# One semaphore per k-and-v buffer for the gathers of a graph attention kernel, in place of eight shared in turn

## The chip, the core and the metric

The kernel runs on one core of one Trainium2 chip. The metric is the device time of one execution in microseconds (us); lower is better. The engines of the core are named as in the profile: PE is the matrix engine's matmul side and PEld its weight loads, DVE is VectorE, ACT is ScalarE, POOL is GpSimd and SP is SyncE. Each engine runs its own instructions in order. Engines and transfers (DMAs) tell each other of finished work through semaphores: a counter that a finished instruction or transfer raises, and that another instruction waits for. A transfer raises its semaphore by 16 in all when it has landed.

## What is computed

A graph with 6250 nodes of 128 features and 206250 edges, sorted by receiver. For each edge, a weight vector comes out of two small networks on its 32 + 32 features; the query of its receiver, that weight and the key of its sender make one attention number for each of 8 heads; this scales the sender's value; the scaled values are summed by receiver, added to the node features and normalized.

```python
w_ij = jax.nn.silu(edge_feats @ rad_W1 + rad_b1) @ rad_W2 + rad_b2
w_ij = w_ij + (jax.nn.silu(chi_scalar @ sph_W1 + sph_b1) @ sph_W2 + sph_b2)
q_i = (node_feats @ Wq).reshape(-1, NUM_HEADS, HEAD_DIM)[receivers]
k_j = (node_feats @ Wk).reshape(-1, NUM_HEADS, HEAD_DIM)[senders]
alpha = (q_i * w_ij * k_j).sum(axis=-1) / jnp.sqrt(jnp.float32(HEAD_DIM))
alpha = alpha * cutoffs[:, None]
v_j = (node_feats @ Wv)[senders].reshape(-1, NUM_HEADS, HEAD_DIM)
out = jax.ops.segment_sum(alpha[..., None] * v_j, receivers, num_segments=n_nodes) / 16.0
x = _layernorm(x + out.reshape(-1, 128), axis=-1)
```

## The kernel before

**Work units.** 128 edges are a tile, four tiles are a quad (512 edges), four quads are a group. There are 403 quads. One execution first computes k and v of all nodes on PE and stores them as a table in memory (`kv_tab`, one row of 1 KB for each node), then runs one loop over the groups with four slots each, one quad a slot, written out by hand: what an engine does stands in its queue in the order of the program text.

**Gathers.** For each tile of a quad, POOL issues one indirect transfer that fetches 128 rows of `kv_tab` by the senders' indices (`gather`, L136). The rows of a quad go into one of `RING` = 16 buffers named `kv`. The function `gathers` issues a quad's four, 14 quads ahead in the program text (`AHEAD` = `RING` - 2). Each is also made to wait for a matmul of the quad that is then current ("no gather ahead of TensorE"), which is 14 quads earlier than the quad that it fetches, and a quad's first gather waits until VectorE has read the buffer's earlier content, which is that of 16 quads earlier. The first eight quads do not gather from `kv_tab`: for them 32 gathers fetch rows of x (tile `msg`), and k and v are computed on the spot.

**Row quads.** For 56 quads, spread between the quads 20 and 392 of the order, POOL gathers only three tiles. The 128 rows of the fourth are fetched by 128 transfers of one row each, 64 issued by SP and 64 by ACT (`load_rows`, tile `wide`). These signal one of eight semaphores of their own, `rows_0` to `rows_7`, and VectorE waits once for a quad's full count (L580), with `declare_fence` telling the layer that records the program that this wait stands for all of them.

**Semaphores of the gathers.** The recording layer gives all other transfers that POOL issues one of eight semaphores in turn, called lanes here. Two transfers of a lane are kept from being in flight together: a gather waits until the gather of eight before, on its lane, has landed. In the program before, the fast path has 1510 separate wait instructions on POOL in front of its 1556 gathers; each names a lane, and 389 of them also name a semaphore of VectorE (the buffer's earlier reader) besides. Where VectorE first reads a quad's rows (L583), it waits for the lanes of its four tiles, two to a wait instruction.

**Behind the gathers.** For each quad VectorE multiplies query and key (`multiply`, L583, tile `kq`), multiplies with the weight (L591), sums over each head (L593), scales (L597) and multiplies into the value (`messages`, L610). PE computes the first layers (L524), the query at the edges (L533, tile `pq`), the weight (L566 and L571, tile `pw`) and the sum by receiver (L622). ACT applies the activation (L554). In a slot, PE and ACT work on later quads than VectorE does.

The lines that the change touches, before:

Of the kernel before, what the change touches and what calls it, by code (L numbers as in the profile page):

```python
# [48 lines left out]
RING = 16  # L49
# [20 lines left out]
def gnn_kernel(ctx, tc, x, src, dst, weight, edges, rad_W1, rad_b1, rad_W2, rad_b2,  # L70
# [14 lines left out]
    nc = tc.nc  # L85
# [46 lines left out]
    def quad_of(name, bufs, width=D):  # L132
        return ep.tile([P, QT, width], F32, name=name, bufs=bufs)

    def gather(o, table, index):
        return nc.gpsimd.indirect_dma_start(  # L136
            out=o, out_offset=None, in_=table,
            in_offset=bass.IndirectOffsetOnAxis(ap=index, axis=0))
# [7 lines left out]
    row_done = {}  # L146
    rows_left = {SP: [], ACT: []}
    owed = {SP: 0, ACT: 0}
    row_sems = [tc.alloc_semaphore(f"rows_{n}") for n in range(ROW_SEMS)]
    row_count = [0] * ROW_SEMS  # L150

    def next_rows(engine, n):

        left = rows_left[engine]
        for _ in range(min(n, owed[engine])):
            row = next(left[0], None)
            while row is None:
                left.pop(0)
                row = next(left[0], None)
            row()  # L160
            owed[engine] -= 1
# [5 lines left out]
    def gathers(q, marks=()):  # L167

        kv = quad_of("kv", RING, 2 * D)
        for t in range(QT - 1 if q in row_quads else QT):  # L170
            o = gather(kv[:, t, :], kv_tab, src_i[:, q * QT + t:q * QT + t + 1])
            if marks:
                tc.add_manual_dep(o.ins, marks[t].ins.name, WAIT, reason="no gather ahead of TensorE")
        kv_of[q] = kv

    def load_rows(i):

# [37 lines left out]
    def kv_parts(q, t):  # L215

        if q not in row_quads:
            return [(t, kv_of[q][:, t, :])]
        return [(slice(0, QT - 1), kv_of[q][:, :QT - 1, :]), (slice(QT - 1, QT), row_of[q])]
# [90 lines left out]
    with tc.tile_pool(name="nodes", bufs=1) as nodes, \  # L310
# [154 lines left out]
        n = len(chunks)  # L465
# [45 lines left out]
        for q in order[XQ:AHEAD]:  # L511
            gathers(q)
# [5 lines left out]
    with tc.tile_pool(name="ps", bufs=1, space=PSUM) as pp, tc.tile_pool(name="loop", bufs=1) as lp:  # L518
# [19 lines left out]
        def after(o, mark, reason="one signal of TensorE a quad"):  # L538
            tc.add_manual_dep(o.ins, mark.ins.name, WAIT, reason=reason)
# [36 lines left out]
        def multiply(q, mark=None, t=slice(0, QT)):  # L576
            if t.start == 0:
                kq_of[q] = quad_of("kq", 3)
            if t.start == 0 and q in row_done:
                o = nc.vector.wait_ge(*row_done[q])  # L580
                tc.declare_fence(o.ins, group=f"rows_{q}")
            for u, kv in kv_parts(q, t):
                o = nc.vector.tensor_tensor(kq_of[q][:, u, :], pq_of[q][:, u, :], kv[:, :, :D],  # L583
                                            op=OP.mult)
                if mark is not None:
                    after(o, mark)
# [182 lines left out]
        q_at_edges(order[0])  # L769
        silus(order[1], first_layers(order[1]))  # L770
        multiply(order[0])
        marks = weigh(order[0])
        mark = marks[-1]
        seen = [mark] * 3
        for g in range(NG - 1):
            for slot, j in enumerate((0, 2, 1, 3)):
                q = g * NQ + j
# [29 lines left out]
                if i + AHEAD < len(order):  # L807
                    gathers(order[i + AHEAD], old[-QT:])
                multiply(order[i + 1], mark)
                messages(q, scores(q, marks=marks), marks=marks)  # L810
                if slot == 0:
# [24 lines left out]
                if g == NG - 2 and slot == 0:  # L836
                    wide_one_hots(order[-1])
                    n = nc.values_load(general, min_val=0, max_val=1)
# [20 lines left out]
        part_sums(g - 1)  # L859
        messages(a, scores(a, weighted=False))  # L860
        multiply(b, mark)
        normalize(g - 3, g - 2, sd)
        write_rows(len(written))
# [191 lines left out]
```

## Time and profile before

| | |
|---|---|
| median of three runs | 1994.42 us (1992.89 to 1995.7) |
| the profiled execution's own time | 1990.48 us |
| its span, first to last instruction | 1988.4 us |
| mean granted TensorE clock | 0.933 of full speed |
| busy PE / PEld / DVE / ACT / POOL | 1788.7 / 1494.6 / 1521.5 / 647.0 / 1474.3 us |
| gathers from `kv_tab` / of x | 1524 / 32, 946 / 957 ns of POOL each |

A busy PE is not PE at its peak, since the ends of matmuls are modelled. The grouped lines give, for a kind of instruction, its count, its total busy time, the mean of one in ns, and the time that the engine sat idle just before them, with what most often ended that idle time. Such a releaser is inferred: of the semaphores that an instruction waits for, it is the one that moved last by the profile, and an instruction whose waits were long met can still carry the name of one that happens to move often. In a timeline a row gives start, duration, engine, line, operation and tiles, and in brackets the idle time before it. In a table of windows "(x128)" is the number of instructions in a stretch of time.

### The profile page before, as it was taken

Reading aid. Unit: us, or ns where it says so; the run is one execution under the profiler, and the core shown is the slowest. Engines: PE = TensorE matmul, PEld = TensorE weight load, DVE = VectorE, ACT = ScalarE, POOL = GpSimd, SP = SyncE. Lnnn points to the kernel's source line nnn. Section 1 sums busy time; section 2 is a strip of 40 time slices with the busy share of each in tenths; the row PEclk is TensorE's granted clock in tenths of the full one; section 3 lists DMA queues with packets and bytes.
Section 4 is the critical chain, followed back from the end, with each engine's and each line's share of the span. In section 5 each row is a group of like instructions: output and inputs, shape, how many; then the busy total and the mean of one; then the engine's idle time right before and its main releaser. Section 6 shows DMA issues by size and latency. Waiting matters only on the chain. (4 is left out here: it accounts for less than half of the span.)

```text
span 1988.4 us, 58734 instructions
## 1 busy us (share of the span) xinstructions
PE 1788.7 (90%) x15990; PEld 1494.6 (75%) x15990; DVE 1521.5 (77%) x3411; ACT 647.0 (33%) x1360; POOL 1474.3 (74%) x1566
## 2 busy tenths in 40 slices
PE   9899989889987988989889889989989888988997
PEld 7787877777876777777777777767778777777776
DVE  6788888677877777777777777777777778777787
ACT  3233333332332332332333323323323333333343
POOL 7777766777777777777777777777777777777775
PEclk9899999988999999898999889999889999998998
DMA  9555545555554555555555555555555555555543
GB/s 342 154 151 155 146 146 147 144 150 152 148 155 144 156 157 147 154 151 151 152 147 153 144 155 146 156 145 156 155 145 155 144 154 151 150 154 145 156 142 91
DMA packets 153261, 305.51 MB, mean 154 GB/s; under 512 B 40300, under 2 KB 87260, under 8 KB 152924
## 3 DMA queue, kind: packets, MB, share of 16 engines
q0 software_dynamic: 74176, 201.95, 35.7%
q1 hardware_dynamic: 70080, 95.67, 15.0%
q10 hardware_dynamic: 8668, 4.08, 1.0%
q8 instruction: 127, 2.08, 0.4%
q14 instruction: 210, 1.72, 0.3%
HBM read 288.10 MB, written 13.46 MB: 152 GB/s over the span
## 5 line engine op out<-in xcount | busy, mean ns | idle before, releaser
L136 POOL DMA_INDIRECT kv<-kv_tab,src_i x1524 | 1441.8, 946 | 489.2 <-PE pw L571 185.0
L554 ACT ACTIVATE act<-ph,b 128x512 f32<-128x512 f32 x806 | 553.3, 687 | 1284.4 <-PE pq L533 677.9
L571 PE MATMUL pw<-w,act 128*128 128x128 f32 x6448 | 889.4, 295 | 0.0
L571 PEld LDWEIGHTS pw<-w,act 128*128 128x128 f32 x6448 | 810.4, 204 | 97.1 <-issue 81.7
L524 PE MATMUL ph<-feats,w 32*128 32x512 f32 x1612 | 544.0, 680 | 47.5 <-ACT act L554 46.1
L533 PE MATMUL pq<-q,hotT 32*128 32x128 f32 x3224 | 495.1, 295 | 8.7 <-DVE kq L583 8.6
L583 DVE TENSOR_TENSOR kq<-pq,kv 128x512 f32<-128x512 f32 (+1 forms) x403 | 270.5, 671 | 294.5 <-DMA kv<-kv_tab,src_i 147.6
L533 PEld LDWEIGHTS pq<-q,hotT 32*128 32x128 f32 x3224 | 414.9, 197 | 29.5 <-DVE kq L583 28.1
L593 DVE TENSOR_REDUCE side<-kq 128x32 f32<-128x512 f32 x403 | 280.1, 695 | 42.2 <-PE pw L571 0.5
L610 DVE TENSOR_TENSOR msg<-kv,side 128x512 f32<-128x512 f32 (+1 forms) x404 | 269.9, 668 | 43.2 <-DVE side L597 0.9
L591 DVE TENSOR_TENSOR kq<-pw,kq 128x512 f32<-128x512 f32 x403 | 274.6, 681 | 0.1
L524 PEld LDWEIGHTS ph<-feats,w 32*128 32x128 f32 x1612 | 150.5, 192 | 161.5 <-ACT act L554 94.9
L566 PE MATMUL pw<-brow,onesb 3*128 3x512 bf16 x403 | 160.7, 399 | 0.6 <-DVE kq L591 0.6
L622 PE MATMUL po<-msg,hot 128*32 128x128 f32 x3200 | 158.3, 296 | 0.0
L663 PE MATMUL pq<-part,to 128*128 128x128 f32 x200 | 49.1, 331 | 107.4 <-DVE kq L583 106.9
L663 PEld LDWEIGHTS pq<-part,to 128*128 128x128 f32 x200 | 33.1, 208 | 118.4 <-DVE kq L583 104.0
L597 DVE TENSOR_TENSOR side<-side,scale 128x32 f32<-128x32 f32 x400 | 80.0, 200 | 43.7 <-DVE side L593 1.4
L622 PEld LDWEIGHTS po<-msg,hot 128*32 128x32 f32 x3200 | 73.4, 113 | 38.9 <-issue 5.5
L263 DVE TENSOR_TENSOR hotT<-relb,side 128x512 f32<-128x512 bf16 x101 | 68.8, 681 | 0.0
L268 DVE TENSOR_TENSOR hot<-rel,side 128x512 f32<-128x512 f32 x100 | 68.1, 681 | 0.0
L257 PE MATMUL pq<-wq,xT 128*128 128x128 f32 x200 | 43.0, 299 | 18.9 <-DVE kq L583 18.6
L257 PEld LDWEIGHTS pq<-wq,xT 128*128 128x128 f32 x200 | 32.7, 205 | 23.0 <-DVE kq L583 22.9
(121 smaller groups left out, 823.9 us busy)
## 6 DMA issues: line engine op xcount, KB each, us to landing
wide<-kv_tab SPq DMA_DIRECT2D x3584, 1.0 KB
wide<-kv_tab ACTq DMA_DIRECT2D x3584, 1.0 KB
feats<-in_edges SPq DMA_DIRECT2D x101, 512.0 KB
kv<-kv_tab,src_i POOLq DMA_INDIRECT x1524
relb<-rel_lin SPq DMA_DIRECT2D x101, 128.0 KB
x<-in_x SPq DMA_DIRECT2D x101, 64.0 KB
out<-y SPq DMA_DIRECT2D x101, 64.0 KB
kv_tab<-kv SPq DMA_DIRECT2D x12, 512.0 KB
```

Of the source, the lines that this page charges most:

```text
L136: return nc.gpsimd.indirect_dma_start(out=o, out_offset=None, in_=table, in_offset=bass.IndirectOffsetOnAxis(ap=index, axis=0))
L524: return nc.tensor.matmul(act_of[q, i], w1[r0:r0 + R, :], feats_of[g][r0:r0 + R, c0:c0 + EQ], start=True, stop=True)
L533: o = nc.tensor.matmul(pq_of[q][:, t, :], hotT_of[g][b, t * P:(t + 1) * P], q_of[g][b, :], start=True, stop=True)
L554: o = nc.scalar.activation(act, act_of[q, i], AF.Silu, bias=b1[:, i:i + 1])
L566: nc.tensor.matmul(pw, onesb, brow.rearrange("p t d -> p (t d)"), start=True, stop=False)
L571: o = nc.tensor.matmul(pw[:, t, :], act_of[q, i][:, t * P:(t + 1) * P], w2[:, i, :], start=False, stop=(t == QT - 1 and i == 1))
L583: o = nc.vector.tensor_tensor(kq_of[q][:, u, :], pq_of[q][:, u, :], kv[:, :, :D], op=OP.mult)
L591: nc.vector.tensor_tensor(m, pw_of[q][:, t, :], m, op=OP.mult)
L593: o = nc.vector.tensor_reduce(alpha, m.rearrange("p t (h e) -> p t h e", e=HD), AX.X, OP.add)
L610: o = nc.vector.tensor_tensor(msg_of[q][:, u, :].rearrange("p t (h e) -> p t h e", e=HD), kv[:, :, D:].rearrange("p t (h e) -> p t h e", e ...
L622: o = nc.tensor.matmul(po_of[g][j * W:(j + 1) * W, :], hot_of[g][:, j * QT + t, :], msg_of[g * NQ + j][:, t, :], start=(t == 0), stop=(t = ...
L663: nc.tensor.matmul(ph[:, :D], to[:n, 0, :], part[:n, :], start=True, stop=(g == 0))
```

## The change

Each of the 16 `kv` buffers gets a semaphore of its own, `kv_0` to `kv_15`. All gathers of a quad raise its buffer's semaphore by 16 each, and they take no lane: the recording layer neither gives them one of its eight semaphores nor follows what depends on their landing. In their place VectorE waits once, ahead of a quad's first multiplication, until the buffer's semaphore has reached the count of the quad's last gather, as it does for the row transfers.

```diff
+    kv_sems = [tc.alloc_semaphore(f"kv_{n}") for n in range(RING)]
+    kv_count = [0] * RING
+    kv_done = {}
...
     def gathers(q, marks=()):
 
         kv = quad_of("kv", RING, 2 * D)
+        n = len(kv_done) % RING
         for t in range(QT - 1 if q in row_quads else QT):
             o = gather(kv[:, t, :], kv_tab, src_i[:, q * QT + t:q * QT + t + 1])
+            tc.no_tile_sem_insts.add(o.ins.name)
+            tc.add_to_no_dep_group(f"kv_{q}", o.ins)
+            o.then_inc(kv_sems[n], 16)
+            kv_count[n] += 16
             if marks:
                 tc.add_manual_dep(o.ins, marks[t].ins.name, WAIT, reason="no gather ahead of TensorE")
         kv_of[q] = kv
+        kv_done[q] = kv_sems[n], kv_count[n]
...
         def multiply(q, mark=None, t=slice(0, QT)):
             if t.start == 0:
                 kq_of[q] = quad_of("kq", 3)
-            if t.start == 0 and q in row_done:
-                o = nc.vector.wait_ge(*row_done[q])
-                tc.declare_fence(o.ins, group=f"rows_{q}")
+            for name, done in (("rows", row_done), ("kv", kv_done)):
+                if t.start == 0 and q in done:
+                    o = nc.vector.wait_ge(*done[q])
+                    tc.declare_fence(o.ins, group=f"{name}_{q}")
```

In the program as built, the order of the working instructions and of the transfers is the same on every engine; only waits differ. On POOL's fast path the separate wait instructions go from 1510 to 393. 379 of those that are left stand ahead of a quad's first gather and name two semaphores of VectorE: that of its engine, as before, and that of its queue, raised when the new wait of 16 quads earlier has passed. No gather from `kv_tab` waits for another gather any more. On VectorE, the lane waits ahead of L583 (734 that name two lanes and 56 that name one) give way to 395 waits for a `kv` semaphore, each of which raises the queue's own semaphore when met, and 395 waits for that one.

## The prediction, as put on record before the changed kernel was run

> **What bounds the kernel now.** I read the page first, then POOL's gathers stretch by stretch and one by one, then VectorE's waits.
>
> ```profile
> span 1988.4 us, 58734 instructions
> PE 1788.7 (90%) x15990; PEld 1494.6 (75%) x15990; DVE 1521.5 (77%) x3411; ACT 647.0 (33%) x1360; POOL 1474.3 (74%) x1566
> L136 POOL DMA_INDIRECT kv<-kv_tab,src_i x1524 | 1441.8, 946 | 489.2 <-PE pw L571 185.0
> L583 DVE TENSOR_TENSOR kq<-pq,kv 128x512 f32<-128x512 f32 (+1 forms) x403 | 270.5, 671 | 294.5 <-DMA kv<-kv_tab,src_i 147.6
> ```
>
> By the first line of busy times PE looks like the bound. But POOL's 74% hides something: 946 ns busy and 489.2 us / 1524 = 321 ns idle make 1.27 us for each gather, and 1556 of these (with the 32 of x) fill the whole span. The next rows are single gathers of POOL's timeline: the first three of all, then the first and the last of the final 20.
>
> ```profile
> 2.88 1.10 POOL L136 DMA_INDIRECT msg<-in_x,src_x  x1 [1.27 <-DMA src_x<-in_src]
> 4.28 0.94 POOL L136 DMA_INDIRECT msg<-in_x,src_x  x1 [0.30 <-issue]
> 5.53 0.95 POOL L136 DMA_INDIRECT msg<-in_x,src_x  x1 [0.30 <-issue]
> ...
> 1949.24 0.94 POOL L136 DMA_INDIRECT kv<-kv_tab,src_i  x1 [0.30 <-issue]
> ...
> 1973.00 0.94 POOL L136 DMA_INDIRECT kv<-kv_tab,src_i  x1 [0.30 <-issue]
> ```
>
> From 1949.24 to 1973.00 there are 19 steps: 1.2505 us each. The first gathers go at the same 1.25, so 0.95 of work and 0.30 of pause belong to a gather itself. 1555 steps of 1.2505 are 1944.5 us; from 2.88 to 1973.00 they took 1970.1. So POOL runs at its own pace from start to end, and lost only 25.6 us on the way. Is it what the others wait for? The first table counts gathers, the second L591, one for each quad.
>
> ```profile
> core 0: us, POOL busy (x), PEclk, DMA share, GB/s
> 70.00:230.00 160.00, 121.10 (x128) 0.99 0.52 154
> 230.00:455.00 225.00, 158.38 (x168) 0.93 0.51 147
> 455.00:900.00 445.00, 335.36 (x356) 0.94 0.52 151
> 900.00:1400.00 500.00, 375.17 (x397) 0.93 0.52 150
> ```
>
> ```profile
> 100.00:230.00 130.00, 21.11 (x31) 0.99 0.52 153
> 900.00:1400.00 500.00, 70.05 (x103) 0.93 0.52 150
> ```
>
> Early, while gathers are far ahead, a quad takes 130 / 31 = 4.19 us. Later it takes 500 / 103 = 4.85, and POOL's 1524 / 395 = 3.86 gathers a quad take 3.86 x 1.2505 = 4.82. VectorE then waits for rows (147.6 us at L583, above). So POOL sets the end; the 14.5 us from the last gather's end (1973.94) to 1988.4 are the last quads' work.
>
> **Where POOL's 25.6 us went.** In 70 to 230 nothing is lost (160 / 1.2505 = 128). In 230 to 455 there is room for 179.9 gathers and there are 168: 11.9 x 1.25 = 14.9 us. Two kinds of gap show. The first:
>
> ```profile
> 316.40 0.95 POOL L136 DMA_INDIRECT kv<-kv_tab,src_i  x1 [0.31 <-issue]
> ...
> 328.16 0.94 POOL L136 DMA_INDIRECT kv<-kv_tab,src_i  x1 [1.53 <-DMA kv<-kv_tab,src_i]
> ```
>
> These two are eight gathers apart, so of one lane, and the later one waited for a landing: the gather that POOL had finished issuing at 317.35 (316.40 + 0.95) had landed only shortly before 328.16. Eight gathers at 1.25 are 10.0 us, and a landing that takes longer stops POOL. The second kind:
>
> ```profile
> 282.71 0.95 POOL L136 DMA_INDIRECT kv<-kv_tab,src_i  x1 [3.28 <-DVE to L653]
> 424.50 0.95 POOL L136 DMA_INDIRECT kv<-kv_tab,src_i  x1 [1.00 <-PE pw L571]
> 958.87 0.94 POOL L136 DMA_INDIRECT kv<-kv_tab,src_i  x1 [1.71 <-DVE side L593]
> 1092.94 0.94 POOL L136 DMA_INDIRECT kv<-kv_tab,src_i  x1 [1.77 <-PE pw L571]
> 1226.52 0.94 POOL L136 DMA_INDIRECT kv<-kv_tab,src_i  x1 [1.16 <-DVE msg L610]
> 1492.69 0.94 POOL L136 DMA_INDIRECT kv<-kv_tab,src_i  x1 [1.17 <-DVE kq L583]
> 1626.52 0.94 POOL L136 DMA_INDIRECT kv<-kv_tab,src_i  x1 [1.53 <-issue]
> 1760.37 1.02 POOL L136 DMA_INDIRECT kv<-kv_tab,src_i  x1 [1.37 <-PE pw L571]
> ```
>
> From 958.87 on these stand 133.6 to 134.1 us apart, or twice that: every 106 gathers, which are 212 instructions of POOL with the wait in front of each. They follow the instruction count, so I read them as POOL's queue fetching its next block. Their pauses sum to 13.0 us, 10.6 beyond 8 x 0.30. The same step seen back from 282.71 falls at 149, in the stretch that lost nothing: with early landings POOL's queue has instructions prepared ahead and a fetch passes unseen. It hurts where the lane wait holds the queue back until just before the gather. That is an inference; the regular step is not.
>
> The rest, 25.6 - 10.6 = 15.0, is longer gathers and lane waits. The first gather alone is 0.15 over 0.95; I leave 1.0 for such and count 14.0 as lane waits.
>
> **The change, part by part.** The wait instructions on POOL (1510 to 393):
>
> ```profile
> L136 POOL DMA_INDIRECT kv<-kv_tab,src_i x1524: 940/946/1468, 43.3 to 1973.0; - x191
> L136 POOLq EVENT_SEMAPHORE  x1510: 17/17/43, 37.9 to 1966.1; - x189
> ```
>
> (ns: least, median, most.) At 17 ns beside a gather that runs they cost nothing, and the pause of 0.30 doesn't come from them: the first one stands at 37.9, while gathers from 4.28 on already go at 1.25. So the steady pace stays; I take 0 for it.
>
> Lane waits go: gain 14.0 us; at least the 14.9 of the early stretch less its two block fetches (3.28 + 1.00 - 0.60 = 3.7), so 11.2; at most 15.0.
>
> Block fetches: POOL's instructions a gather fall from 2 to about 1.25, so if each still cost what it does, 10.6 x 0.375 = 4.0 is gained; if the queue is far enough ahead, as before 230, all 10.6. I take 10.6, since nothing is left that holds the queue: the buffer's earlier reader is 16 quads back and the matmul 14.
>
> [...]
>
> VectorE: the waits at L583 remain two, but the second now waits for the first.
>
> ```profile
> L593 DVE TENSOR_REDUCE side<-kq 128x32 f32<-128x512 f32 x403 | 280.1, 695 | 42.2 <-PE pw L571 0.5
> L580 DVEq EVENT_SEMAPHORE  x56: 21/21/21, 170.6 to 1925.8; - x56
> ```
>
> L593 waits for VectorE's own L591, idle 42.2 / 403 = 0.105 us each: the bound above for one such turn, 395 x 0.105 = 41 us in all. Below it is nothing, since a wait met early passes beside running work, 21 ns as at L580. I take 0.1, but it lies in a quad's slack of 4.82 - 4.19 = 0.63 us, and PE, ACT and POOL don't wait for VectorE to issue gathers. On the path are only the last three quads: 0.3 us. If VectorE set the pace, the cost would be the 41.
>
> Sum: 14.0 + 10.6 - 0.3 = 24.3, from the profiled execution's own 1990.5 to 1966.2. That execution lies 3.9 under the median of 1994.4; carried over, **1970**.
>
> What is late next: quads must then go at 3.86 x 1.2505 = 4.82 without pauses, against 4.19 when fed, so POOL's own 0.95 + 0.30 remains the bound.
>
> **The rivals.**
>
> *Landing is a bound of its own.* The lanes hold POOL only where landings are late; without them more gathers may merely be under way, and VectorE waits at L583 instead. For it: the 10 us landing above, with the 16 transfer engines busy only 0.51 of the time on average.
>
> ```profile
> wide<-kv_tab SPq DMA_DIRECT2D x3584, 1.0 KB
> wide<-kv_tab ACTq DMA_DIRECT2D x3584, 1.0 KB
> ```
>
> A landing so late at half load means that some part of a gather queues behind other traffic, and these 7168 one-row transfers are the candidate. Against it: from 455 on, 1.25 to 1.26 us a gather was landed for over 1400 us. If the early stretch gains nothing, what stays is 14.0 - 11.2 = 2.8, and the six later fetches, 8.7 - 1.8 = 6.9: 9.7 us, so 1985.
>
> [...]
>
> [...]
>
> *Nothing changes.* The waits on POOL show 43 ns at most; were the gaps not the lanes', everything stays: 1994. Against it stands the row at 328.16, with a landing named as releaser and eight rows between.
>
> **How the numbers follow.** Forecast 0.62 (its own range 1965 to 1980, with the fetches' 4.0 to 10.6 and 1.5 of scatter as in the runs shown), landing-bound 0.19, crowding 0.11, nothing 0.08. All told the range is 1963 to 1991: it holds the forecast and nearly all of the landing-bound case, and leaves out crowding and nothing. Faster by over 0.2% (about what a measurement of this kernel tells from no change) 0.81, within it 0.08, slower 0.11.
>
> **What would show it.** In the profile after: POOL's last gather starts near 1949 (not 1973); 230 to 455 holds about 180 gathers; the gaps at every block of instructions are gone or under 0.5 us; the pause stays 0.30. The wait at L583 for landings is no more than now. I am wrong on the cause if POOL finishes early but the end doesn't move, which is the landing bound, or if gaps over 0.30 remain as many as they are, and wrong on VectorE's wait if quads take over 4.85 us while gathers have long landed.

## The result, and the profile after

The changed kernel takes 1966.8 us (median of four runs, 1966.19 to 1967.4) against 1993.89 us before (four runs, 1992.89 to 1995.7): a ratio of 0.9863, 95% interval 0.9846 to 0.988. The forecast was 1970, its own range 1965 to 1980, the whole range 1963 to 1991. The profiled execution took 1966.43 us; the sum of the prediction for it was 1966.2.

From the page of the changed kernel, the span, the busy times and two of the costliest groups (lines below L136 have moved down: the first multiplication is now L593, the second L601, the sum over heads L603):

```profile
span 1964.3 us, 57621 instructions
PE 1770.4 (90%) x15990; PEld 1480.0 (75%) x15990; DVE 1516.8 (77%) x3411; ACT 648.3 (33%) x1360; POOL 1476.0 (75%) x1566
L136 POOL DMA_INDIRECT kv<-kv_tab,src_i x1524 | 1442.6, 947 | 465.0 <-issue 198.8
L593 DVE TENSOR_TENSOR kq<-pq,kv 128x512 f32<-128x512 f32 (+1 forms) x403 | 269.8, 669 | 249.1 <-DVEq L590 110.0
```

The third line is where the time came from: POOL's idle time in front of its gathers fell from 489.2 to 465.0 us, which is 24.2, while a gather kept its length (946 to 947 ns). The last line is where it could have gone and did not: VectorE's wait for gathered rows, which was 147.6 us with the landing named as releaser, is 110.0 with the queue's own semaphore named (the turn behind the new wait at L590); all the idle time ahead of the first multiplication fell from 294.5 to 249.1.

POOL's gathers in the same stretches as before, and VectorE's second multiplication (one for each quad) in two of them:

```profile
core 0: us, POOL busy (x), PEclk, DMA share, GB/s
70.00:230.00 160.00, 121.13 (x128) 0.98 0.53 153
230.00:455.00 225.00, 170.16 (x180) 0.95 0.54 153
455.00:900.00 445.00, 336.34 (x357) 0.93 0.54 153
900.00:1400.00 500.00, 378.08 (x400) 0.93 0.54 152
```

```profile
230.00:455.00 225.00, 33.34 (x49) 0.95 0.54 153
900.00:1400.00 500.00, 70.73 (x104) 0.93 0.54 152
```

In 230 to 455 there are 180 gathers in place of 168, and 225 / 180 = 1.250 us is POOL's own pace. Every stretch now runs at it: 500 / 400 = 1.25. A quad takes 500 / 104 = 4.81 us late in the run, which is POOL's 3.86 x 1.2505 = 4.82 again.

The instructions of L136 (ns: least, median, most; then first and last start), POOL's timeline around the place where before had its longest pause, and the last gather:

```profile
L136 POOL DMA_INDIRECT kv<-kv_tab,src_i x1524: 942/946/1648, 44.2 to 1950.6; - x191
L136 POOLq EVENT_SEMAPHORE  x393: 17/43/43, 39.4 to 1931.5; - x197
```

```profile
281.48 0.95 POOL L136 DMA_INDIRECT kv<-kv_tab,src_i  x1 [0.30 <-PE pw L580]
282.73 0.94 POOL L136 DMA_INDIRECT kv<-kv_tab,src_i  x1 [0.30 <-DVEq L590]
...
1950.56 0.95 POOL L136 DMA_INDIRECT kv<-kv_tab,src_i  x1 [0.30 <-issue]
```

Of the 38 pauses over 0.34 us that POOL had before (24.3 us beyond the 0.30 of each, added up along its timeline) none is left after the first gather. The bracket names change from gather to gather while the number stays 0.30: this is the case in which a releaser is only the semaphore that moved last, and the number says that nothing was waited for.

What the 38 pauses were can be read from the trace of the kernel before, by matching each gather with the increments of its lane's semaphore (a trace lacks some increments; the last one recorded is taken as the landing). No gather there starts less than 0.76 us after the landing of the gather eight before. In 28 of the 38 pauses it starts 0.76 to 0.79 us after it: these are the lane waits, 13.4 us beyond the 0.30 of each. The eight pauses that the prediction lists at every 106th gather start 3.34 to 3.40 us after that landing: 10.6 us. At four further steps of 106 gathers the landing had come early enough for that, at most 5.7 us after the issue, and nothing is lost. Two pauses, 0.3 us together, fit neither (one of them stands at a step of 106). In the changed kernel landings are no earlier: from 455 us on, a quad has landed 6.5 to 7.3 us (medians of three stretches) after POOL's part in its last gather ended, and at most 10.5, where the kernel before has medians of 5.7 to 6.4. POOL no longer waits for them.

### The profile page after: what moved, and what is told of

Its sections match the earlier page's. It is cut to its first block, busy times and chain, and to the rows that moved or that the text cites. A ratio compares the mean times of both kernels' runs of the same rounds, so it can differ in the third digit from the quotient of the medians.

```text
span 1964.3 us, 57621 instructions
## 1 busy us (share of the span) xinstructions
PE 1770.4 (90%) x15990; PEld 1480.0 (75%) x15990; DVE 1516.8 (77%) x3411; ACT 648.3 (33%) x1360; POOL 1476.0 (75%) x1566
## 3 DMA queue, kind: packets, MB, share of 16 engines
q8 instruction: 127, 2.08, 0.5%
## 5 line engine op out<-in xcount | busy, mean ns | idle before, releaser
L136 POOL DMA_INDIRECT kv<-kv_tab,src_i x1524 | 1442.6, 947 | 465.0 <-issue 198.8
L580 PEld LDWEIGHTS pw<-w,act 128*128 128x128 f32 x6448 | 802.0, 203 | 96.3 <-issue 79.0
L542 PE MATMUL pq<-q,hotT 32*128 32x128 f32 x3224 | 487.6, 292 | 5.9 <-DVE kq L593 5.8
L593 DVE TENSOR_TENSOR kq<-pq,kv 128x512 f32<-128x512 f32 (+1 forms) x403 | 269.8, 669 | 249.1 <-DVEq L590 110.0
L542 PEld LDWEIGHTS pq<-q,hotT 32*128 32x128 f32 x3224 | 408.8, 195 | 19.7 <-DVE kq L593 15.5
L603 DVE TENSOR_REDUCE side<-kq 128x32 f32<-128x512 f32 x403 | 279.9, 695 | 43.6 <-DVE kq L601 1.4
L601 DVE TENSOR_TENSOR kq<-pw,kq 128x512 f32<-128x512 f32 x403 | 274.1, 680 | 0.6 <-PE pw L580 0.6
L673 PE MATMUL pq<-part,to 128*128 128x128 f32 x200 | 48.8, 330 | 95.6 <-DVE kq L593 93.2
L673 PEld LDWEIGHTS pq<-part,to 128*128 128x128 f32 x200 | 33.7, 212 | 105.1 <-DVE kq L593 90.2
L272 DVE TENSOR_TENSOR hotT<-relb,side 128x512 f32<-128x512 bf16 x101 | 68.7, 681 | 0.0
L690 DVE TENSOR_TENSOR y<-tot,x 128x128 f32<-128x128 f32 x98 | 28.2, 287 | 27.3 <-DMA out<-y 27.3
```

The source lines that it names most:

```text
L136: return nc.gpsimd.indirect_dma_start(out=o, out_offset=None, in_=table, in_offset=bass.IndirectOffsetOnAxis(ap=index, axis=0))
L542: o = nc.tensor.matmul(pq_of[q][:, t, :], hotT_of[g][b, t * P:(t + 1) * P], q_of[g][b, :], start=True, stop=True)
L580: o = nc.tensor.matmul(pw[:, t, :], act_of[q, i][:, t * P:(t + 1) * P], w2[:, i, :], start=False, stop=(t == QT - 1 and i == 1))
L601: nc.vector.tensor_tensor(m, pw_of[q][:, t, :], m, op=OP.mult)
L603: o = nc.vector.tensor_reduce(alpha, m.rearrange("p t (h e) -> p t h e", e=HD), AX.X, OP.add)
L673: nc.tensor.matmul(ph[:, :D], to[:n, 0, :], part[:n, :], start=True, stop=(g == 0))
```

## The experiments

Four sets of runs were made, each beside runs of the kernel before on the same chip. In two sets (e1 to e4, and e9 and e10) the kernel before took 1991.4 and 1993.6 us, as at first. In the other two (e5 to e8, and e11 and e12) it took 2655.1 and 2663.8, with another bound; what they still tell comes last. The runs' times are medians.

**e1 and e2: take away what makes landings late.** The same edit on the kernel before (e1) and on the changed one (e2). It makes every quad gather four tiles, so that no one-row transfer is issued and POOL issues 56 gathers more:

```diff
-    row_quads = {order[i] for i in row_at}
+    row_quads = set()
...
     def load_rows(i):
 
+        return
```

Expected of e1:

> The kernel before, with the one-row transfers of SP and ACT left out: POOL gathers the fourth tile of the 56 row quads too, 1612 gathers in all. Theory (POOL's pace of 1.2505 us sets the end, and what cost 24 us were landings that came more than eight gathers late, because a part of each gather queues behind the one-row transfers): landings are prompt, the lane waits and the block fetches cost nothing, and the last gather starts near 2.9 + 1611 x 1.2505 = 2017; with some 14.5 us behind it and 2 around the span, 2035, give or take 4. Rival (the gain came from fewer wait instructions on POOL, or from one wait in place of two on VectorE): the eight shared semaphores cost here what they cost with the one-row transfers, so 2035 + 24 = 2059.

Expected of e2:

> The changed kernel with the one-row transfers left out in the same way, 1612 gathers. Theory: 2035, give or take 4, and within 3 us of the kernel before without these transfers: the change gains nothing where landings are prompt. Rival (fewer waits are the gain): 2035, and 24 us under the kernel before without these transfers.

Measured: e1 2035.53 us, e2 2035.28 us, both at a ratio of 1.0222 (1.0205 to 1.0239) to the kernel before: the theory's 2035, and neither rival's 24 us between the two. From e1, the old semaphores with prompt landings, the instructions of L136 and two stretches; then the gathers of e2:

```profile
L136 POOL DMA_INDIRECT kv<-kv_tab,src_i x1580: 942/946/2088, 43.9 to 2019.1; - x198
L136 POOLq EVENT_SEMAPHORE  x1566: 17/17/231, 37.2 to 2012.0; - x196
```

```profile
230.00:455.00 225.00, 170.28 (x180) 0.95 0.50 148
900.00:1400.00 500.00, 378.09 (x400) 0.94 0.50 146
```

```profile
L136 POOL DMA_INDIRECT kv<-kv_tab,src_i x1580: 942/946/1451, 43.4 to 2017.9; - x198
```

With 1566 wait instructions and eight lanes, POOL runs at its own pace, 180 gathers in 225 us, and has no pause over 0.34 us. Landings are prompt there: from the end of POOL's part to the last increment of a gather's semaphore it takes 1.9 us at the median and 4.2 at most after 60 us, where the kernel before has 6.2 at the median, and 7.8 and up to 10.7 in 255 to 392 us (matched as above). So neither the lanes nor the number of waits cost anything by themselves: the two kernels differ by 27 us only while one-row transfers delay landings. Added to the changed kernel, 56 x 1.2505 = 70.0 us make 2036.8, close to the 2035.28 of e2. The pauses at every 106th gather are gone from e1 too, with about two instructions of POOL to a gather as before: such a step passes unseen when landings are early. The prediction had inferred this, and e1 shows it. That what happens at the step is a fetch of instructions, with others prepared ahead, remains a reading of the count of instructions: the page of the kernel before lists two DMA queues of the kind "instruction" (127 packets, 2.08 MB, and 210 packets, 1.72 MB), but no view here ties a packet of theirs to a step.

**e4: give the instructions back, without anything to wait for.** All but the first of a quad's gathers get a wait for a quad eight back, which is long met:

```diff
         for t in range(QT - 1 if q in row_quads else QT):
+            if t and len(kv_done) >= 8:
+                nc.gpsimd.wait_ge(*list(kv_done.values())[-8])
             o = gather(kv[:, t, :], kv_tab, src_i[:, q * QT + t:q * QT + t + 1])
```

> The changed kernel, with a wait added on POOL in front of each gather but a quad's first, on the landing of the quad of eight before (some 40 us ago, met long since): again two instructions of POOL a gather, as before the change, but nothing to wait for. Theory (block fetches are hidden where nothing holds the queue): 1967, give or take 1.5. Rival (the fetches cost by the number of instructions): about 10 us more, 1977, with pauses of over 1 us every 106 gathers. Rival (each wait instruction costs): 1991.

Measured: 1966.45 us (1965.05 to 1968.12), ratio 0.9872 (0.9855 to 0.9888). The added waits of e4, and its gathers:

```profile
L176 POOLq EVENT_SEMAPHORE  x1105: 17/17/17, 77.9 to 1935.4; - x185
L136 POOL DMA_INDIRECT kv<-kv_tab,src_i x1524: 942/946/2092, 44.0 to 1950.6; - x191
```

1105 waits of 17 ns each beside running gathers, and POOL's last gather starts at 1950.64, within 0.1 us of the kernel after. Fewer instructions on POOL are not the gain.

**e3, e9, e10: put a limit back, at three depths.** POOL is held at the start of each quad until an earlier quad has landed in full: the third before (e3), the fourth (e9) or the second (e10). The edit of e3, which the others repeat with -4 and -2:

```diff
         kv = quad_of("kv", RING, 2 * D)
         n = len(kv_done) % RING
+        if len(kv_done) >= 3:
+            nc.gpsimd.wait_ge(*list(kv_done.values())[-3])
```

Expected of e3. (The last gather of the third quad before is the ninth before, not the eighth, where the quads between have four tiles each.)

> The changed kernel, with one wait added on POOL in front of each quad's first gather: until the quad of three before has landed in full, whose last gather is the eighth before. This is the limit of the eight lanes, by one instruction a quad and without touching VectorE. Theory: the loss comes back for the most part, 10 to 25 us: 1977 to 1992, in pauses over 0.30 on POOL. Rival (wait instructions, or VectorE's wait): 1967 to 1968.

Expected of e9. (It counts one quad too few: between the fourth quad before and the present one stand 12 gathers, so the landing has 13 steps, about 16 us, and not 11. The theory's number stays, since more room holds nothing either.)

> The same kernel as e5_brake12, again, on a chip where the kernel before takes about 1991. Theory (a limit on gathers under way costs only what the landing is later than the limit allows): the last gather of the quad waited for is 8 to 9 steps of 1.25 us back, about 11 us, landings are at most about 10.4 us late, so nothing is held: 1967 plus or minus 2, no pause on POOL over 0.5 us. Rival (what was gained is that POOL waits for no landing at all, whatever the depth): 1971 or more. Where the kernel before takes 2650 again, POOL isn't the bound and nothing follows.

Expected of e10:

> The same kernel as e6_brake4, again, on a chip where the kernel before takes about 1991. Theory: the last gather waited for is about 5 steps (6.3 us) back, landings take 6 to 8 us at the median, so a quad loses 0 to 3 us at its start from 230 us on: slower than the 1991 of before, between 2000 and 2400, with some hundred pauses on POOL. Rival (the lanes' cost in the kernel before was not the landing): 1967 to 1980.

Measured, with the pauses over 0.34 us added up along POOL's timeline in the profiled execution, beyond 0.30 each (a row quad of three tiles in between takes a step from what e3, e9 and e10 allow):

| kernel | steps that a landing has | pauses | us lost in them | time, us | ratio to before |
|---|---|---|---|---|---|
| e10 | 5, once a quad | 83 | 68.7 | 2038.18 | 1.0228 (1.0207 to 1.0249) |
| before | 8, at every gather | 38 | 24.3 | 1993.89 | 1 |
| e3 | 9, once a quad | 19 | 9.2 | 1976.01 | 0.9921 (0.9904 to 0.9937) |
| e9 | 13, once a quad | 0 | 0 | 1970.79 | 0.9887 (0.987 to 0.9903) |
| after | no limit | 0 | 0 | 1966.80 | 0.9863 (0.9846 to 0.988) |

One pause from the timeline of e3 and two from that of e10, and the gathers of both:

```profile
576.70 0.94 POOL L136 DMA_INDIRECT kv<-kv_tab,src_i  x1 [1.59 <-issue]
```

```profile
210.16 0.95 POOL L136 DMA_INDIRECT kv<-kv_tab,src_i  x1 [4.08 <-issue]
...
222.98 0.95 POOL L136 DMA_INDIRECT kv<-kv_tab,src_i  x1 [3.10 <-issue]
```

```profile
L136 POOL DMA_INDIRECT kv<-kv_tab,src_i x1524: 940/946/2088, 44.0 to 1959.5; - x191
```

```profile
L136 POOL DMA_INDIRECT kv<-kv_tab,src_i x1524: 943/949/1642, 43.7 to 2022.5; - x191
```

The stretch 230 to 455 and the one from 900 in e10, and the instructions of L136 in e9:

```profile
230.00:455.00 225.00, 153.79 (x163) 0.95 0.48 141
900.00:1400.00 500.00, 369.95 (x391) 0.91 0.51 149
```

```profile
L136 POOL DMA_INDIRECT kv<-kv_tab,src_i x1524: 944/949/2078, 44.1 to 1955.0; - x191
L136 POOLq EVENT_SEMAPHORE  x772: 17/43/6917, 39.2 to 1935.8; - x193
```

The shorter the allowance, the more of the landing shows up on POOL, and the end follows: e10 lost 68.7 us in pauses and ended 67.4 above e9 on the same chip, and 71.4 above the kernel after. The releaser named at the three pauses shown is "issue", but the landing of the quad waited for stands 0.75 to 0.76 us before the start of the gather at 16 of the 19 in e3 and 74 of the 83 in e10. At 13 steps POOL's engine is not held: its queue waited up to 6.9 us at a time in e9, while the engine still had gathers to work on.

e9 missed its forecast of 1967 plus or minus 2, and stands 0.2 us under the rival's 1971; what decides against the rival is that no pause is left. The 4.0 us over the kernel after are not pauses: in its profile a gather takes 949 ns at the median in place of 946 (e10 has 949 too), and 1556 x 3 ns are 4.7 us. By the ratios, whose intervals overlap, e9 and the kernel after are not told apart. e3 came out 1.0 us under the range that was expected, e10 inside its wide one, with fewer pauses than the some hundred expected and the first at 169 us instead of 230. In e10 landings came sooner: a quad has landed 3.4 us after its last gather at the median from 455 us on, where the kernel before has 5.7 to 6.4. So the row transfers alone do not set how late a landing is; how many gathers are under way seems to count too, which no run here separates.

**The two sets with another bound: e5 to e8, e11 and e12.** e5 and e6 are the kernels of e9 and e10. e7 and e11 are one kernel, the changed one with VectorE's wait for a quad's rows given five times:

```diff
                 if t.start == 0 and q in done:
                     o = nc.vector.wait_ge(*done[q])
                     tc.declare_fence(o.ins, group=f"{name}_{q}")
+                    for _ in range(4):
+                        nc.vector.wait_ge(*done[q])
```

e8 and e12 are the changed kernel with more row quads, so fewer gathers on POOL and more one-row transfers on SP and ACT:

```diff
-ROW_TILES = 56
+ROW_TILES = 72
```

and 60 in e12. Expected of e5, e6, e7 and e8, in this order (for e5, what is waited for is the fourth quad before, not the third, as said for e9):

> The kernel after, with POOL held at the start of each quad until the quad three before it has landed (12 gathers at most under way at that point, 9 at least ahead of the one waited for). Theory (a limit on gathers under way costs only what the landing is later than the limit allows): the last gather of the quad waited for is 8 to 9 steps of 1.25 us back when a later quad's first is due, about 11 us, and landings are at most about 10.4 us late, so nothing is held: 1967 plus or minus 2, with no pause on POOL over 0.5 us. Rival (what was gained is that POOL waits for no landing at all, whatever the depth): a part of the loss returns, 1971 or more.

> The kernel after, with POOL held at the start of each quad until the quad two before it has landed in full, so that the last gather waited for is some 5 steps (6.3 us) back at most. Theory: median landings of 6 to 8 us no longer fit, so a quad loses some 0 to 3 us at its start from 230 us on, where row transfers run: between 1990 and 2400, many hundred waits on POOL, more than the 1994 of before. Rival (the lanes' cost in the kernel before was not the landing): 1967 to 1980.

> The kernel after, with each quad's wait on VectorE for its rows given five times in place of once. Theory (VectorE's waits lie in a quad's slack of about 0.6 us, POOL sets the pace): 1967 plus or minus 2. Rival (the wait for the queue's own semaphore costs about 0.1 us a quad on the path): each added turn of it costs up to 41 us, so at least 10 us more, 1977 or above.

> The kernel after, with 72 row quads in place of 56: 16 gathers fewer on POOL, 2048 one-row transfers more on SP and ACT. Theory (POOL's 1.25 us a gather is still the bound): 16 x 1.25 = 20 us less, 1947 plus or minus 4. Rival (landing is the next bound: the one-row transfers delay a part of every gather, and more of them delay it more): 1960 or more, with VectorE waiting longer at its first multiplication.

Expected of e11 and e12:

> The same kernel as e7_more_dve_waits, again, on a chip where the kernel before takes about 1992. Theory (VectorE's waits lie in a quad's slack of about 0.6 us, POOL sets the pace): 1967 to 1971, as the runs on such chips so far. Rival (a wait on VectorE costs about 0.1 us a quad on the path that sets the end): 41 us or more over that, 2008 or above; half of it, 1988, would count for it too.

> The kernel after, with 60 row quads in place of 56: four gathers fewer on POOL, 512 one-row transfers more. Theory (POOL's 1.25 us a gather is the bound of the kernel after, and nothing else stands close to it): 5 us less than the kernel after, 1962 to 1966. Rival (SP's queue, which in the profile after stands idle for only some 5 per cent of the time between 400 and 1800 us, fills up with the added 256 transfers and loads): no gain or some us slower, 1967 to 1985, with the output of quads or the edge loads issued later.

Measured: beside 2655.09 us for the kernel before, e5 2635.35, e6 2634.15, e7 2644.78, e8 3018.41; beside 2663.75, e11 2655.47 and e12 2711.14. From e5, the busy times, a late stretch of POOL's gathers, and the instructions of SP's one-row transfers; then one line of the latter from the changed kernel at first (ns: least, median, most):

```profile
PE 2177.8 (83%) x15990; PEld 1778.4 (68%) x15990; DVE 1526.9 (58%) x3411; ACT 652.9 (25%) x1360; POOL 1472.2 (56%) x1566
```

```profile
900.00:1400.00 500.00, 286.77 (x304) 0.81 0.39 116
```

```profile
L205 SPq MOVE wide<-kv_tab x3584: 1/29/1003, 193.9 to 2551.2; - x200
L205 SPq DMA_DIRECT2D wide<-kv_tab x3584: 2/227/1598, 194.0 to 2551.9; - x200
```

```profile
L203 SPq MOVE wide<-kv_tab x3584: 29/29/38, 110.9 to 1866.4; - x200
```

From the timelines at 1000 us, a run of SP's one-row transfers in e5 and one in the changed kernel, and from the page of e8 the shares by engine of the chain that ended last:

```profile
1000.18 4.94 SPq L205 DMA_DIRECT2D wide<-kv_tab  x9
```

```profile
1003.44 3.58 SPq L203 DMA_DIRECT2D wide<-kv_tab  x10
```

```profile
PE 36%; SPq 26%; issue 20%; ACTq 9%; DVE 4%; another core or an unknown queue 2%; DMA 1%; ACT 1%; DVEq 0%
```

POOL issues 304 gathers in 500 us in place of 400, so it is not the bound there; a limit at 4 or at 12 gathers is one and the same (e5 and e6). SP's simple instructions, 29 to 38 ns in the changed kernel at first, take up to 1003 here, though 29 at the median still; nine rows take 4.94 us (0.55 each) where ten took 3.58 (0.36), and SP stands on the chain of e8. Over the whole trace a row follows the one before on SP after 0.53 us on average in e5 and 0.35 in the changed kernel, while on ACT it is 0.35 in both. Row quads then cost instead of gaining: e12 lies 55.7 us over e11 for four of them, 14 each (e11 has four more waits a quad on VectorE besides), and e8 by the ratios (1.1368 - 0.9931) x 2655 = 382 us over e5 for sixteen, 24 each. All this makes SP a likely bound, but does not show it: PE is slower too, with 331 ns for a matmul of the weight (tile `pw`) at a mean granted clock of 0.82, where the changed kernel had 293 at 0.942, and PE is the releaser named most at the waits of POOL's gathers and of VectorE's first multiplication. What slowed SP isn't known. It isn't the chip alone: e11 and e12 ran on the chip of e1 to e4. So whether four more waits on VectorE would cost anything when POOL is the bound, and whether more row quads then gain, was not decided: no theory of e5 to e8, e11 and e12 met its time, and where a rival's open range holds the time, it is for this other bound; they stay open. The changed kernel itself was not run in these two sets. e7 and e11, which are the changed kernel with four added waits a quad, are at 0.9965 (0.9947 to 0.9983) and 0.9958 (0.9937 to 0.998) of the kernel before, so no loss there either. No run beat the changed kernel beyond its scatter.

## Why the prediction was right

**POOL as the bound: right.** POOL's last gather was to start near 1949 and starts at 1950.56; the end moved with it, in the kernel after and in e3, e9 and e10. The stretch of 180 gathers, the pause of 0.30 and the wait at the first multiplication came as said.

**Pauses, 14.0 of lane waits and 10.6 at the regular step: right in both amounts, 24.6 against the 24.2 us by which POOL's idle time fell.** By the landings in the trace of the kernel before, the lane waits are 13.4 us and the eight regular pauses 10.6. e1 shows that the regular part needs late landings and e4 that the number of instructions alone does not bring it; e10, e3 and e9 show that what held POOL was the allowance for the landing. One step of the reading was loose: at the regular pauses the lane's landing did not come just before the gather but 3.34 us before it, with only 0.76 needed elsewhere. So a landing that is well inside its eight steps can still cost there.

In the kernel before, eight of the regular pauses cost 0.7 to 3.0 us beyond the usual 0.30; in e1, e4 and the kernel after no such pause is seen. That these pauses are fetches of blocks of instructions, as the prediction read them, was not shown.

**The rest of the sum was right partly by luck.** POOL's last gather came 22.4 us earlier (1973.00 to 1950.56), not 24.6 less anything. Its idle time fell by 24.2, but its gathers were 0.8 longer in all (1441.8 to 1442.6), and the first one from the table came at 44.2 instead of 43.3: 24.2 - 0.8 - 0.9 = 22.5. The prediction had put such at 1.0 us for the kernel before and nothing for the difference. Against that the end after the last gather shrank from 14.4 to 12.8 us. The eight kernels profiled at the usual pace show either 12.8 (the kernel after, e1, e9) or 14.0 to 14.4 (before, e2, e3, e4, e10), whichever semaphores they use; e4 has the kernel after's POOL end and 14.4. So 1.6 us of the agreement are scatter, and that the profiled time came within 0.2 us of the sum is luck.

**VectorE's 0.1 us a turn, 0.3 on the path, 41 at most: the size was about right, and it does not set the end.** Where a landing ended VectorE's wait, the first multiplication starts 0.123 us at the median after the last increment in e1 (125 cases) and 0.204 in e2 (250 cases), 0.204 too in the changed kernel (104). So the added turn costs 0.08 us there, and 395 of them would be 32 us; e1 and e2 end 0.25 us apart. Late quads take 4.81 us, POOL's pace. The 0.3 us at the end can't be seen beside 1.6 of scatter. e7 and e11, which were to price more such turns, fell into the two sets where POOL was not the bound. One premise was too strong, that PE and POOL don't wait for VectorE: a quad's first gather waits for VectorE's read of 16 quads earlier, and PE waited 93.2 us in all for the first multiplication at one line of the changed kernel (L673). What holds is that none of this reached POOL, which shows no pause over 0.34 us.

**The rivals.** *Landing is a bound of its own* (1985) fell: the wait at the first multiplication went down, 147.6 to 110.0, with the transfer engines moving 153 GB/s in 230 to 455 in place of 147. *Crowding* (slower, 0.11) fell with it: with no lane to limit the gathers under way, none of the stretches shown is slower than before. The reading that one-row transfers make landings late was right (1.9 us at the median without them in e1, 6.2 in the kernel before), and the error would have been to take a late landing for a slow one: with 16 buffers and 14 quads of room, landings up to 10.5 us late cost nothing here, as POOL did not wait for them. Where a gather's part waits behind these rows was not shown: no view here tells which transfer engine a row took. *Nothing changes* (1994) fell with the result, 27 us under the kernel before.

## What to carry to other kernels

Where an engine sets the end with work of its own and still pauses, compare the pauses with the distance between an instruction and the one that it is made to wait for: eight steps of 1.25 us were too short for landings of up to 10.7 us, thirteen were enough. A releaser's name can mislead ("issue", or an engine); the time since the landing that is waited for, 0.76 us again and again, does not. A limit on transfers under way cost here by what landings exceeded it (68.7 us of pauses at 5 steps, 9.2 at 9, none at 13), so give the limit the depth of the buffers, not that of a pool of semaphores. Before counting wait instructions as a cost, add met ones: 1105 of them cost nothing here.

## What was not expected of the hardware

The kernel before, on a chip that had run it at 1991 us, took 2664 in a later set of runs. In that set SP's 29 ns instructions took up to 1507 ns in e12's trace, and the granted clock was 0.81 in 900 to 1400, where the kernel before had 0.93. A gather took 948 ns of POOL at the mean in e12, against 946 in the kernel before, with POOL's pace set elsewhere (292 gathers in 900 to 1400, against 397). The length of a gather is 946 ns at the median in the kernels before and after and in e1 to e4, and 949 in e9 and e10, and it is not the chip that decides: e5, with a mean of 945, and e6, with 948, ran on one chip in one set. What decides it isn't known.
